# Turning an attention mask over in one transposing transfer instead of four, in a planned two-layer graph-attention kernel

## The chip, the cores and the metric

The kernel runs on one core of one Trainium2 chip. The metric is device time in microseconds (us) for one launch, the median of three timed runs. Five engines work side by side and are ordered only by semaphores: PE (TensorE, matrix products), DVE (VectorE), ACT (ScalarE), POOL (GpSimd) and SP (SyncE, which here only issues transfers). Matrix products read SBUF and write PSUM; DMA engines move data between HBM and SBUF, and within SBUF.

## The reference

There are 32 independent graphs of 512 nodes with 512 features, each with its own 512x512 adjacency matrix. Layer 0 is one head of graph attention, layer 1 holds two (four heads of 256 features, then one of 512); both have a layer norm and a relu in front and add to their input.

```python
h = relu(layernorm(x))                                  # layer 0
scores = leaky_relu(h@w_src [:,None] + h@w_dst [None,:] + b)
scores = where(adj + eye == 0, -inf, scores)
x = x + softmax(scores, -1) @ h

h = relu(layernorm(x))                                  # layer 1
def gat_layer(x, mask, W, a_src, a_dst, bias):
    xl = x @ W                                          # per head
    e = leaky_relu(asrc[:, None] + adst[None, :])       # [source, target]
    e = where(mask, e, -1e9)
    return softmax(e, axis=source).T @ xl + bias
h = elu(gat_layer(h, mask, W1, ...))                    # 4 heads x 256, side by side
x = x + gat_layer(h, mask, W2, ...)                     # 1 head x 512
```

Every softmax needs the mask twice: once with the node that is summed over along the free axis, to find each target's largest score, and once with it on the partitions, to mask the weights that the matrix product takes. So each graph's mask is used in both orientations, in both layers (layer 0 and layer 1 prepare masks of their own).

## The kernel before

A graph's nodes lie on the 128 partitions in `T` = 4 blocks; most tiles are 128 x 4 x 512. All 32 graphs go through the same steps, and a graph's layer 0 is worked on while the graph before it is in layer 1.

**The planner.** Nothing is issued directly. Each step is entered with `op(engines, cost, emit, reads, writes, ahead, lock)` (L60) in the order of the program text. `Plan.run` (L88) then makes schedules ("drafts") in Python before the kernel is built, and emits the instructions in the order of the best one. A draft (L132) is a list schedule: each engine takes, of the steps whose inputs are ready by the plan's own costs, the one of lowest rank. The rank of step i is at first `i - ahead` (L86): `AHEAD` = 400 pulls a step forward, `-LATER` = -300 puts it back. After a draft, `latest` (L112) works out how late each step could have been, and that is the rank for the next draft; up to `DRAFTS` = 6 are made in this chain, and the one with the earliest end by the plan's own costs is kept. `lock` marks steps on DVE and POOL that the plan does not overlap. Costs stand in `on_dve`, `on_pool`, `by_dma`, `by_turning` and so on (L234 to L264). On the chip each engine runs its instructions strictly in the planned order, and waits on semaphores.

**The masks.** `masks0` (L719) loads a graph's adjacency matrix with one POOL-issued transfer (`load_adj`, L706) that casts to bf16, turns it into 0 or a large negative number on DVE (L726, L729), and has it turned over by `transposed_mask` (L711): four transposing transfers issued from SP (L715), one for each block of 128 source nodes. `masks1` does the same for layer 1 (L741, L747). The buffers are `m0`, `m0T`, `m1`, `m1T` (128 x 4 x 512, bf16). In `edge_weights` (L625) DVE adds a mask row to the scores and takes the maximum (L634; with `m0` in layer 0, with `m1T` in layer 1), PE spreads that maximum over the partitions (L497), ACT makes the scores `E` (L655), DVE subtracts the maximum (L658), POOL adds the other mask (L660; `m0T` in layer 0, `m1` in layer 1) and ACT takes the exponential (L663). The products of `E` with the values are `aggregate` (L666, PE at L673).

**Rows by way of HBM.** A score vector is turned into a row on all partitions by a PE transpose (L596), a copy (L530), a transfer to HBM (`lines<-row`, L602) and a broadcasting transfer back (`row<-lines`, L612), both on SP's queue, then sometimes a copy to PSUM (L622).

**The projections** (`products`, L816, PE at L868) multiply in quarters by a seven-product scheme. Their weights are four quarters and four combinations T1, T2, T3, -T4 of them, made once in `sums` (L473, instructions at L480 and L481) after the weights have come in and after `scores_1` and `scores_2` (L439, L452, DVE dots at L383) have put two score columns beside each quarter. `weights_of` (L486) tells which pieces a product waits for.

**The beginning and the end.** The first lines of the plan (L1043 on) load graph 0's features, the constants, and go through layer 0 of graph 0. At the end, `EARLY` = T // 2 = 2 of the four output blocks of the last graph but one are entered ahead of the last graph's heads (L1060), the other two behind its last projection (L1076), and then the last graph's own output.

## Time and profile before

| | |
|---|---|
| median of 3 timed runs | 3653.59 us (3653.02 to 3653.67) |
| the profiled execution | 3651.96 us, of which 3650.2 us lie between its first and last instruction (the span) |
| mean granted TensorE clock | 0.993 |
| PE busy | 3534.9 us, 97% of the span |
| DVE busy | 2870.0 us, 79% |
| ACT busy | 2253.6 us, 62% |
| POOL busy | 1494.5 us, 41% |
| transposing transfers of masks | 256, four for each of 64 masks, 131 KB each |
| transposing transfers of head outputs (`turned`, L556) | 192, 262 KB each |

Times in the profile are counted from the first instruction. A group line names the source line, the engine, the operation, what it writes and reads, its shape and how often it ran, then its busy time in us and the mean ns of one, then how long the engine stood idle just before such instructions and what ended that. PE is the engine that is busy nearly all of the time.

### The profile page before, as it was taken

The numbers are of one execution on the slowest core, as the hardware profiler recorded it, in microseconds if no ns is written. First come the engines' busy times: TensorE is split into PE (matmuls) and PEld (weight loads), VectorE is DVE, ScalarE is ACT, GpSimd is POOL, SyncE is SP. The second block draws the span as 40 slices with busy tenths as digits, with TensorE's granted clock in tenths as the row PEclk, the third lists the DMA queues.
The fourth block names the chain that finished last, engine by engine and source line by source line (L and its number), as shares of the span: only waits on it lengthen the run. The fifth ranks groups of instructions, "written<-read, shape, count | busy, mean of one in ns | idle before, by whom it ended". The sixth has DMA issues, their size and how long they took to land.

```text
span 3650.2 us, 50711 instructions
## 1 busy us (share of the span) xinstructions
PE 3534.9 (97%) x16852; PEld 3039.1 (83%) x16852; DVE 2870.0 (79%) x7341; ACT 2253.6 (62%) x3929; POOL 1494.5 (41%) x1297
## 2 busy tenths in 40 slices
PE   4899999999999999999999999999999999999998
PEld 3688888888888888888888888888888888888877
DVE  7978778878778887778787788777787877887855
ACT  2666566665666665666656566656666656666554
POOL 4534334434334443344343344343343433443422
PEclk9999999999999999999999999999999999999999
DMA  6244333444333443434443344443344433334321
GB/s 165 72 116 116 99 100 103 94 128 113 95 94 105 104 122 105 96 96 105 116 115 100 93 104 99 124 111 92 98 110 105 118 99 101 101 99 122 102 76 40
DMA packets 516519, 378.85 MB, mean 104 GB/s; under 512 B 354488, under 2 KB 393120, under 8 KB 516256
## 3 DMA queue, kind: packets, MB, share of 16 engines
q1 hardware_dynamic: 482464, 342.06, 33.2%
q0 software_dynamic: 33792, 33.56, 6.5%
q8 instruction: 132, 2.16, 0.2%
q14 instruction: 131, 1.07, 0.1%
HBM read 257.16 MB, written 68.01 MB: 89 GB/s over the span
## 4 chain that ended last, share of the span: by engine, by line
PE 75%; DVE 12%; POOL 4%; ACT 2%; issue 2%; DMA 1%; SPq 1%; DVEq 0%; POOLq 0%; ACTq 0%
PE acc L673 42%; PE acc L868 28%; DVE junk L383 4%; PE acc L497 4%; POOL E_one L660 4%; DVE junk L634 2%; DVE E L849 1%; ACT acc L622 1%; DVE E_one L658 1%; DVE hT L536 1%; DMA row<-lines 1%; DVE col L512 1%; ACT h L520 1%; PE acc L596 1%; SPq L715 1%
## 5 line engine op out<-in xcount | busy, mean ns | idle before, releaser
L673 PE MATMUL acc<-pair,E 128*128 128x257 f32 x4096 | 915.9, 379 | 2.8 <-ACT E L663 2.8
L673 PEld LDWEIGHTS acc<-pair,E 128*128 128x128 f32 x4096 | 771.2, 189 | 115.7 <-ACT E L663 3.2
L660 POOL TENSOR_TENSOR E<-E,m 128x512 f32<-128x512 f32 x512 | 619.7, 1239 | 461.7 <-DVE E L658 451.4
L868 PE MATMUL acc<-w_T,E 128*128 128x257 f32 (+1 forms) x2048 | 526.3, 381 | 5.3 <-POOL w_T L481 5.3
L673 PE MATMUL acc<-h,E_one 128*128 128x256 f32 (+1 forms) x2048 | 485.8, 381 | 9.1 <-ACT E_one L663 6.5
L634 DVE CUSTOM_DVE_ANT_0 junk<-m1T,acc 128x512 bf16<-128x512 bf16 x640 | 435.7, 681 | 30.3 <-ACT acc L622 14.9
L673 PE MATMUL acc<-xl,E_one 128*128 128x257 f32 x1984 | 447.8, 380 | 3.9 <-ACT E_one L663 3.3
L868 PEld LDWEIGHTS acc<-w_T,E 128*128 128x128 f32 x2048 | 384.5, 190 | 63.8 <-POOL w_T L481 5.7
L673 PEld LDWEIGHTS acc<-h,E_one 128*128 128x128 f32 x2048 | 379.6, 190 | 64.2 <-ACT E_one L663 8.5
L881 DVE TENSOR_TENSOR pair<-acc,pair 128x258 f32<-128x258 f32 (+1 forms) x390 | 165.8, 426 | 330.8 <-PE acc L868 285.7
L673 PEld LDWEIGHTS acc<-xl,E_one 128*128 128x128 f32 x1984 | 370.1, 190 | 58.8 <-ACT E_one L663 8.6
L663 ACT ACTIVATE E<-E 128x512 f32<-128x512 f32 x512 | 314.8, 621 | 123.2 <-POOL E L660 123.1
L530 ACT COPY pair<-acc 128x258 f32<-128x258 f32 (+1 forms) x456 | 168.9, 371 | 314.1 <-PE acc L868 308.8
L655 ACT ACTIVATE E<-row,ac 128x512 f32<-128x512 f32 x512 | 340.4, 709 | 32.9 <-DMA row<-lines 32.3
L658 DVE TENSOR_TENSOR E<-E,acc 128x512 f32<-128x512 f32 x512 | 327.5, 676 | 13.1 <-PE acc L497 12.7
L530 ACT COPY xl<-acc 128x257 f32<-128x257 f32 x220 | 81.3, 370 | 388.5 <-PE acc L868 388.5
L660 POOL TENSOR_TENSOR E_one<-E_one,m0T 128x512 f32<-128x512 f32 x128 | 144.7, 1154 | 339.6 <-DVE E_one L658 339.6
L709 POOL DMA_DIRECT2D m<-in_adj_dram x64 | 51.5, 804 | 540.5 <-DVE col L634 493.7
L868 PE MATMUL acc<-w,hT 128*128 128x258 f32 x1024 | 267.7, 382 | 0.0
L868 PE MATMUL acc<-w,E 128*128 128x257 f32 (+1 forms) x1024 | 258.0, 380 | 0.0
L941 DVE SCALAR_TENSOR_TENSOR v<-acc,r,b_r 128x256 f32<-128x256 f32 x512 | 241.8, 478 | 9.0
L868 PE MATMUL acc<-w,pair 128*128 128x257 f32 x1024 | 248.3, 379 | 0.0
(114 smaller groups left out, 6167.2 us busy)
## 6 DMA issues: line engine op xcount, KB each, us to landing
row<-lines SPq DMA_DIRECT2D x442, 256.0 KB
m<-in_adj_dram POOLq DMA_DIRECT2D x64, 512.0 KB, 5.8
x<-in_x_dram SPq DMA_DIRECT2D x32, 1024.0 KB
spill<-x SPq DMA_DIRECT2D x32, 1024.0 KB
x<-spill SPq DMA_DIRECT2D x32, 1024.0 KB
out_dram<-x SPq DMA_DIRECT2D x30, 1024.0 KB
v<-row SPq DMA_TRANSPOSE x192
m0T<-m SPq DMA_TRANSPOSE x128
```

Source lines behind the costliest of these rows:

```text
L383: nc.vector.scalar_tensor_tensor(junk[:, : vector.shape[1]], values, 1.0, vector, op0=ALU.mult, op1=ALU.mult, accum_out=out)
L497: op("PE", on_pe(P, transpose=True), lambda: nc.tensor.transpose(dst_of(), src_of(), identity), src, dst(part), ahead)
L530: nc.scalar.copy(dst_of(), src_of())
L634: lambda t=t: nc.vector.tensor_tensor_reduce(junk, mask_max.at[:, t, :], a_row.at, 1.0, LOWEST, ALU.add, ALU.max, accum_out=amax.at[:, t : ...
L655: lambda t=t: nc.scalar.activation(E.at[:, t, :], c_row.at, AF.Prelu, bias=a_of(t), scale=1.0, alpha=SLOPE),
L658: op("DVE", on_dve(N), lambda t=t: nc.vector.tensor_sub(E.at[:, t, :], E.at[:, t, :], m_row.at), m_row(*ROW) + E(t), E(t))
L660: "POOL", on_pool(N, True), lambda t=t: nc.gpsimd.tensor_add(E.at[:, t, :], E.at[:, t, :], mask.at[:, t, :]),
L663: op("ACT", on_act(N), lambda t=t: nc.scalar.activation(E.at[:, t, :], E.at[:, t, :], AF.Exp), E(t), E(t))
L673: lambda s=s: nc.tensor.matmul(acc.at[:, :n], E.at[:, s, node_block(t)], of(s), start=(s == 0), stop=(s == T - 1)),
L868: lambda k=k: nc.tensor.matmul(acc.at[:, :width], at[a]()[:, k, node_block(r)], weight_of(w, k, c), start=(first and k == 0), stop=(k == n ...
L881: op("DVE", on_dve(width), lambda: nc.vector.tensor_add(place(), acc.at[:, :width], place()), acc(0) + token, token)
L941: lambda i=i, v=v, acc=acc, r=r: nc.vector.scalar_tensor_tensor(v.at[:, i, :], acc.at[:, :F], r.at, b1_r[:, h * F : (h + 1) * F], op0=ALU. ...
```

## The change

It has six parts.

1. `transposed_mask` turns the whole 128 x 2048 mask with one transfer (both callers pass `True`). The result then lies in another order: of each 128-column block of the turned mask, the four source blocks are no longer side by side. `mask_row` picks the row out as four pieces of 128, and the two users (L634, L660) get their operands as 128 x 4 x 128 by `by_blocks`.
2. `load_adj` keeps every later adjacency load waiting for the first one to have landed (`START`), and its planned costs differ for the first three.
3. `load_x(0)` gets a higher rank, ahead of the constants.
4. `sums` is made in two pieces: the weight values as soon as the weights are in, and the two score columns (8 elements a partition for W1) when the dots are done. That is eight instructions for each of the two weight matrices instead of four.
5. `EARLY` is 1: one block of the last graph but one is entered ahead of the last graph's heads, three behind its projection.
6. The planner keeps `ahead` apart from `i` and tries six multiples of it (0.25 to 1.5), and makes two drafts of each (one by the rank, one by `latest`) in place of a chain of up to six.

```diff
-    DRAFTS = 6
+    AHEAD, DRAFTS = (0.25, 0.5, 0.75, 1.0, 1.25, 1.5), 1
...
-        self.ops.append((engines, cost, emit, after, bufs, i - ahead, lock))
+        self.ops.append((engines, cost, emit, after, bufs, (i, ahead), lock))
...
-        rank, best = [o[5] for o in self.ops], None
-        for _ in range(self.DRAFTS):
-            draft = self.draft(rank)
-            if draft is None:
-                break
-            if best is None or draft.end < best.end:
-                best = draft
-            rank = self.latest(draft)
+        best = None
+        for part in self.AHEAD:
+            draft = self.draft([i - part * ahead for i, ahead in (o[5] for o in self.ops)])
+            for _ in range(self.DRAFTS):
+                if draft is not None and (best is None or draft.end < best.end):
+                    best = draft
+                draft = draft and self.draft(self.latest(draft))
...
-    def sums(w, name, kinds, n, later):
+    def sums(w, name, nk, kinds, n, later):
-        for dst, a, b_ in (("T3", "22", "T1"), ("T1", "T1", "11"), ("T2", "22", "T1"), ("-T4", "21", "T2")):
-            token = {q: W[name](*((q, *kind) for kind in kinds)) + W[name]((q, "done")) for q in FACTORS}
...
+        for part, cols in (("values", slice(2, None)), ("columns", slice(0, 2))):
+            token = {
+                q: W[name]((q, part), *((q, k) for k in range(nk)), *((q, *kind) for kind in kinds if part == "columns"))
+                for q in FACTORS
+            }
+            for dst, a, b_ in (("T3", "22", "T1"), ("T1", "T1", "11"), ("T2", "22", "T1"), ("-T4", "21", "T2")):
+                width = n if part == "values" else 16
...
     def weights_of(name, kinds):
-        return lambda q: W[name](*((q, *kind) for kind in kinds)) + W[name]((q, "done"))
+        return lambda q: W[name](*((q, *kind) for kind in kinds), (q, "values"), (q, "columns"))
...
-                    junk, mask_max.at[:, t, :], a_row.at, 1.0, LOWEST, ALU.add, ALU.max, accum_out=amax.at[:, t : t + 1]
+                    by_blocks(junk), mask_row(mask_max, t), by_blocks(a_row.at), 1.0, LOWEST, ALU.add, ALU.max,
+                    accum_out=amax.at[:, t : t + 1],
...
-                "POOL", on_pool(N, True), lambda t=t: nc.gpsimd.tensor_add(E.at[:, t, :], E.at[:, t, :], mask.at[:, t, :]),
+                lambda t=t: nc.gpsimd.tensor_add(by_blocks(E.at[:, t, :]), by_blocks(E.at[:, t, :]), mask_row(mask, t)),
...
+    START, adj_loads = Buffer(None), []
...
-            (), xb(*((t, half) for t in range(T) for half in range(2))),
+            (), xb(*((t, half) for t in range(T) for half in range(2))), 0 if b else 2 * AHEAD,
...
-        op("POOL", (2200.0, 8000.0), lambda: nc.gpsimd.dma_start(m.at, node_tiles(adj, b)), (), m(*ROW))
-    def transposed_mask(m, mT):
-        for t in range(T):
+        first, early = not START.wrote, len(adj_loads) < 3
+        adj_loads.append(b)
+        op(
+            "POOL", (1100.0, 5500.0) if first else (2200.0, 16000.0 if early else 8000.0), lambda: nc.gpsimd.dma_start(m.at, node_tiles(adj, b)),
+            () if first else START(0), m(*ROW) + (START(0) if first else []),
+        )
+    def transposed_mask(m, mT, whole=False):
+        for t in (None,) if whole else ROW:
             op(
-                "SP", by_turning(2 * P * N),
-                lambda t=t: nc.sync.dma_start(mT.at[:, :, node_block(t)], m.at[:, t, :], transpose=True),
-                m(t), mT(t),
+                "SP", by_turning(2 * P * N * (T if whole else 1)),
+                lambda t=t: nc.sync.dma_start(
+                    mT.at.rearrange("p a (b n) -> p (a b) n", n=P) if whole else mT.at[:, :, node_block(t)],
+                    m.at.rearrange("p t n -> p (t n)") if whole else m.at[:, t, :], transpose=True,
+                ),
+                m(*ROW) if whole else m(t), mT(*ROW) if whole else mT(t),
             )
+    def by_blocks(row):
+        return row.rearrange("p (b n) -> p b n", n=P)
+    def mask_row(mask, t):
+        if mask.kind in ("m0T", "m1T"):
+            return mask.at.rearrange("p a (b n) -> p a b n", n=P)[:, :, t, :]
+        return by_blocks(mask.at[:, t, :])
...
-    EARLY = T // 2
+    EARLY = 1
```

## The prediction

> **What bounds the kernel now.** I read the busy shares first, then busy time by stretch, then PE's waits, then the timeline of the beginning, one graph in the middle and the end.
>
> ```profile
> PE 3534.9 (97%) x16852; PEld 3039.1 (83%) x16852; DVE 2870.0 (79%) x7341; ACT 2253.6 (62%) x3929; POOL 1494.5 (41%) x1297
> ...
> 0.00:60.00 60.00, 20.35 (x76) 15.90 (x76) 43.38 (x143) 9.15 (x13) 14.10 (x22) 1.00 0.90 208
> 60.00:120.00 60.00, 39.67 (x151) 31.59 (x152) 54.33 (x140) 24.75 (x51) 34.12 (x20) 0.74 0.32 91
> 120.00:200.00 80.00, 77.49 (x373) 66.89 (x372) 67.97 (x174) 51.93 (x86) 37.24 (x31) 1.00 0.26 73
> ...
> 1000.00:1500.00 500.00, 494.89 (x2374) 427.24 (x2373) 401.37 (x1025) 320.62 (x550) 209.31 (x182) 1.00 0.40 104
> ...
> 3600.00:3650.20 50.20, 39.31 (x171) 32.61 (x169) 14.39 (x34) 7.48 (x16) 6.63 (x6) 0.90 0.06 21
> ```
>
> In the stretches the columns are length, busy PE, weight loads, DVE, ACT, POOL, then granted clock, DMA share, GB/s. The number of matrix products is not changed, so time can only come from PE's idle time, 3650.2 - 3534.9 = 115 us, and from stretches at a low clock. Of the 115, 39.6 + 20.3 = 60 us lie in the first 120 us, 2.5 us up to 200 us, about 34 us in the 3200 us up to 3400, and 19 us behind that. So the beginning is the largest pool, the middle is a small loss per graph times some 29 graphs, and the end is third.
>
> PE's waits say what ends last in each. First the beginning (up to 120 us), then the middle (120 to 3400):
>
> ```profile
> PE acc L497 <- DVE junk L383: 24.9, 4, 21.7
> PE acc L497 <- DVE col L641: 8.4, 2, 4.3
> PE acc L868 <- POOL w_T L481: 5.3, 1, 5.3
> PE acc L868 <- DVE pair L881: 5.0, 1, 5.0
> ...
> PE acc L497 <- ACT acc L622: 26.0, 26, 1.2
> PE acc L596 <- DVE ac L766: 4.2, 22, 0.5
> ```
>
> Columns: total us, times, longest. In the beginning PE waits for DVE, which is 90 to 100% busy in each 10 us slice from 20 to 80 us; DVE itself can't start before the features are there. In the middle there is one recurring gap of about 1 us a graph. None of PE's long waits in the middle names a mask's landing; in all waits together DVE's L634 waits 1.5 us, in 2 instances, for L715. The four-transfer turning is already hidden there, so part 1 can pay only through what it takes from SP's queue and by letting the plan be laid out differently.
>
> **Part 1, one transfer for four.** The two transposing rows have different sizes, 131 KB and 262 KB:
>
> ```profile
> L715 SPq DMA_TRANSPOSE m0T<-m x128: 1192/1259/2693, 24.5 to 3325.6; - x128
> L715 SPq DMA_TRANSPOSE m1T<-m x128: 1188/1194/3186, 35.8 to 3538.6; - x128
> ...
> L556 SPq DMA_TRANSPOSE v<-row x192: 1231/1232/2468, 134.2 to 3589.9; - x192
> ```
>
> These are min/median/max ns that SP spends on one. Twice the bytes cost 40 ns more, so four times cost some 120 ns: 1.3 us (estimate from these rows). SP spends 4 x 1.25 = 5.0 us on a mask now and 1.3 us after, 2 x 3.7 = 7.4 us less a graph. The data: the quiet 262 KB transfer issued at 262.45 us moves nothing up to 263.60 and has the DMA engines full (228 GB/s) from 263.60 to 264.75; a quiet 131 KB one keeps them at 0.81 for 0.70 us (187 GB/s). So 0.6 us and 1.1 us, hence about 2.0 us for the whole mask, and landing 1.2 + 2.0 = 3.2 us after issue, where the fourth of four lands 3 x 1.26 + 1.2 + 0.6 = 5.6 us after the first issue. Gain 2.4 us in the mask's own latency, hidden in the middle. The row transfers behind it on SP's queue (L612, which release ACT's L622 and L655) can go out up to 3.7 us sooner, but stand behind 2.0 us of data and not 0.6.
>
> The strided operands: L634 takes 681 to 685 ns (768 of them), L660 with m0T 1154 ns (128 of them). No row shows the same instruction with four pieces of 128. The nearest are DVE's and POOL's sums at L849 and L850, whose operands are two pieces of 256: on hT DVE takes 676 ns, the same as the unbroken L658 (676), and POOL's 1306 to 1487 stands beside 1288 for the unbroken L796. So I take 0 on both, with bounds of 0 and 0.2 us on each of 128 POOL instructions (POOL is 41% busy, so it costs only where a chain waits), and 0 to 30 ns on DVE: 768 x 0.03 = 23 us on an engine with 780 us free.
>
> In the middle, the recurring gap is at L497 (the spread of the maximum), for example 1.09 us before 553.43. There L641 took 0.80 us instead of 0.15 and L639 1.01, while POOL's four L660 ran from 548.75 to 553.25; ahead of that DVE's first L634 with m1T started at 545.92, released by L622 (0.60 us idle), whose row left SP at 542.56 behind the four m1T transfers of 535.78 to 542.45. With one transfer that row can leave about 3 us sooner, and the maximum can be done before POOL's block begins. If so 26 x 1.0 = 26 us go; if the new order puts DVE's instructions as they are now, nothing; if it makes another such gap, 26 to 30 us come. Between ends of -28 and +28 I take -8, about a third of the gain, because the gap depends on DVE's order, which follows the plan and not the transfer.
>
> **Parts 2 and 3, the beginning.** DVE idles until x lands:
>
> ```profile
> DVE st L503 <- DMA x<-in_x_dram: 12.4, 1, 12.4
> ...
> 0.00:5.00 5.00, 0.00 (x0) 0.00 (x0) 0.25 (x4) 0.00 (x0) 3.31 (x13) 1.00 0.57 87
> 5.00:10.00 5.00, 0.00 (x0) 0.00 (x0) 0.00 (x0) 0.00 (x0) 0.00 (x0) 1.00 1.09 242
> 10.00:14.00 4.00, 0.00 (x0) 0.00 (x0) 0.02 (x1) 0.00 (x0) 0.00 (x0) 1.00 1.13 314
> ```
>
> By 14 us the queues had moved 5 x 87 + 5 x 242 + 4 x 314 KB = 2.9 MB, of which x is 1.05 MB. Beside it ran three adjacency loads (0.52 MB each as written) and two constant rows (0.26 MB each). With x first (0.75 instead of 2.14 us) and one adjacency load beside it, 1.57 MB are to be moved. The same curve reaches that at 9.7 us, 1.4 us of which go with the earlier issue: x lands at about 8.3, 5.7 us sooner than the 13.98 at which DVE starts now. DVE is full from 20 us on, so its whole sequence moves up if its other inputs are in time. I take -5 us, bounds 0 (another load is late instead: w1 and the attention vectors, whose dots fill DVE from 35 to 62 us) and -7. The later adjacency loads wait on POOL's queue until the first has landed; behind them there stand only L904 and, at 17.28 us, L507. DVE takes the layer-1 mask at 18.94 us now, but its first reader (L634) comes at 107.31, and the second layer-0 mask at 55.26.
>
> **Part 4, the sums.** Now L481 runs on POOL at 70.27, 76.39 and 80.82 (2.8 us each) and PE stands 5.34 us until 79.25 for it; the eight products that follow took 3.81 us and not 1.74, in a slice with clock 0.77. Made from the values alone, the sums can run before DVE's dots end at 65.3. PE saves 5.3 + 2.1 us there, unless DVE is then late with what comes next: it is 96% busy in that slice. The four column pieces add four instructions of about 0.1 us each, per matrix. DVE's dots beside POOL took 1.6 to 2.7 us instead of 0.69 from 67 to 84 us, and one beside the first L481 took 2.46 at 43.77; that blocking is moved into the dots, not removed. I take -4, bounds -8 and +3.
>
> The Trainium skill, "SBUF — State Buffer", says in its part on the port that DVE and GpSimd share that a vector instruction with two SBUF inputs and a GpSimd instruction that reads SBUF exclude each other for their whole length; that agrees with the 2.46 us above and speaks against part 4: by it the sums only exchange places with dots, DVE gains nothing, and the part would be worth 0 instead of -4, the time 3639.
>
> **Part 5, the end.** PE is idle 10.9 us in the last 50, mostly 3.0 us before 3626.08 and 2.7 us before 3629.94, while the last maximum is taken. One block is 16 products of 0.22 us, 3.5 us of filler. But filler runs wherever PE would wait, and DVE is 88 to 98% busy from 3550 to 3580, so some goes there. I take -2, bounds -3.5 and +1.
>
> **Part 6, the drafts.** It costs nothing itself. It decides the order, and so is in the bounds of the middle.
>
> Sum: -8 - 5 - 4 - 2 = -19 us on the profiled 3651.96: 3633. The median of the timed runs stands 1.6 us above the profiled execution: 3634.6, so 3635.
>
> **The rivals.** *The middle's gap goes whole*: L497's 26 us vanish, -26 - 11 = -37: 3617. For it: the gap is one and the same in 26 graphs, so one change of order removes all. Against: two releasers stand within 0.1 us of each other before 553.43 (L641 and L622), and both must move. *The beginning is hidden*: DVE is full anyway and its dots, blocked by POOL, end when they did; the middle stays: -2 to -3, 3651. For it: DVE's load in the first 120 us is 98 us. Against: 12.4 us of its idle time are the wait for x. *Slower, the new draft leaves a second gap*: only one refinement follows each start now, where six were chained. A second stall like L497's, 1.09 us in each of 28 graphs, is +30.5, less 11 from beginning and end: +19.5, 3673. It decides from 11 / 28 = 0.4 us a graph, and is slower by over 0.2% from 0.65. For it: middle gaps come from order alone, and the plan's costs don't hold such blocking of small DVE steps. Against: twelve drafts are compared, the first two of the old chain among them.
>
> **How the numbers follow.** Chances: forecast 0.49 (own range 3622 to 3646), the gap gone 0.17, hidden 0.16, slower 0.18. 0.2% is 7.3 us, about what a measurement of this kernel can tell from no change. Faster 0.49 + 0.17 = 0.66, same 0.16, slower 0.18. The range reaches from 3606 (gap gone and the better bounds of beginning and end) to 3664 (a second gap of some 0.75 us a graph); most of the slower rival is left out.
>
> **What would show it.** Right: BN_STATS starts near 8.3 us; the wait of L868 for L481 is gone; 64 transfers at L715 of about 1.3 us; L634 stays near 683 ns; L622 releases PE less. Wrong: L634 over 720 ns, PE idle over 1.6 us a graph in the middle, or the first L673 product later than 35 us (38.80 now).

## The result

| | before | after |
|---|---|---|
| median of 12 timed runs, side by side | 3652.94 us (3652.00 to 3654.26) | 3648.74 us (3645.19 to 3651.69) |
| span of the profiled execution | 3650.2 us | 3646.7 us |
| SP's time on the mask's transfers, each (median) | 4 x 1.19 to 1.26 us | 1.62 us (`m0T`), 3.03 us (`m1T`) |

The ratio is 0.9989, interval 0.9981 to 0.9996: 4.2 us or 0.11% faster. The interval lies just below 1, but one short measurement could not tell this from no change, and it is 14 us behind the forecast of 3635. The runs of the changed kernel lie 6.5 us apart, those of the kernel before 2.3.

The busy shares, and busy time by stretch (length, PE, weight loads, DVE, ACT, POOL, granted clock, DMA share, GB/s), of the changed kernel:

```profile
PE 3542.6 (97%) x16852; PEld 3036.1 (83%) x16852; DVE 2851.2 (78%) x7367; ACT 2264.6 (62%) x3929; POOL 1424.6 (39%) x1279
```

```profile
0.00:60.00 60.00, 24.18 (x94) 19.43 (x95) 41.88 (x125) 13.49 (x20) 27.44 (x29) 0.95 0.80 203
60.00:120.00 60.00, 44.44 (x179) 35.23 (x178) 55.30 (x172) 23.33 (x49) 28.16 (x25) 0.85 0.34 100
120.00:200.00 80.00, 72.85 (x339) 60.39 (x338) 66.53 (x167) 50.13 (x82) 34.19 (x29) 0.98 0.25 71
1000.00:1500.00 500.00, 495.13 (x2372) 425.74 (x2372) 401.31 (x1032) 325.42 (x554) 195.56 (x177) 1.00 0.38 103
```

PE is busier in the first 120 us (24.18 + 44.44 = 68.6 us, 60.0 before) and less busy from 120 to 200 (72.85, 77.49 before). In the middle nothing moves (495.13, 494.89 before).

For a sharper count I use PE's **lost time**. Consecutive products of 256 columns or more start 0.2175 us apart when nothing is in the way, those of 128 columns half of that, 0.1088 us; the 16852 products make 3503.1 us in every kernel here, and what a span has above that is lost, to waits, to a low clock or to the last output. It is put down to the stretch in which it falls. Each row is one profiled execution; the ratio is that of the timed runs to those of the kernel before on the same chip.

| kernel | lost, 0 to 200 us | 200 to 3400 | from 3400 | span | ratio (95%) |
|---|---|---|---|---|---|
| before | 78.1 | 43.5 | 25.5 | 3650.2 | |
| after | 76.0 | 43.1 | 24.5 | 3646.7 | 0.9989 (0.9981 to 0.9996) |
| e1: part 1 alone | 82.9 | 44.3 | 23.0 | 3653.2 | 0.9995 (0.9986 to 1.0003) |
| e2: parts 2 and 3 alone | 76.9 | 45.8 | 26.9 | 3652.7 | 0.9993 (0.9984 to 1.0002) |
| e3: part 4 alone | 79.6 | 45.1 | 26.6 | 3654.4 | 1.0002 (0.9993 to 1.0011) |
| e4: part 6 alone | 77.7 | 49.8 | 26.3 | 3657.0 | 0.9995 (0.9986 to 1.0004) |
| e5: first landing planned at 13000 | 75.1 | 38.5 | 23.7 | 3640.5 | 0.9959 (0.9947 to 0.9972) |
| e6: a real wait for the first landing | 77.9 | 42.2 | 22.5 | 3645.8 | one run |
| e7: two blocks held back | 77.6 | 43.3 | 22.0 | 3646.0 | 0.9975 (0.9965 to 0.9985) |
| e8: dots planned longer | 71.6 | 75.0 | 24.6 | 3674.4 | 1.0034 (1.0021 to 1.0046) |
| e9: short dots | 65.5 | 41.9 | 21.7 | 3632.2 | 0.9949 (0.9934 to 0.9964) |
| e10: e5 and e7 | 75.3 | 38.9 | 21.0 | 3638.4 | 0.9946 (0.9933 to 0.9958) |
| e11: part 1 undone, drawn anew | 77.8 | 45.4 | 26.1 | 3652.4 | 0.9993 (0.9984 to 1.0002) |
| e12: first landing planned at 9000 | 74.6 | 30.7 | 22.9 | 3631.3 | 0.9936 (0.9920 to 0.9953) |
| e13: e12's order, four transfers | 75.5 | 79.0 | 26.2 | 3683.9 | 1.0055 (1.0043 to 1.0068) |
| e14: e12 and e7 | 73.3 | 31.0 | 20.8 | 3628.2 | 0.9923 (0.9911 to 0.9936) |
| e15: after's order, four transfers | 77.6 | 56.1 | 25.6 | 3662.4 | 1.0018 (1.0010 to 1.0027) |

So the 3.5 us between the two profiled spans are 2.1 from the beginning, 0.4 from the middle and 1.0 from the end. Some profiled executions lie off their kernel's median: e13's 8.6 us above it, e8's 11.4, e4's 4.4, e5's, e7's and e10's 3, and e9's 3.8 below. So a stretch is read for where the time lies, and what a kernel gains by the ratio.

What ends PE's waits after the change, in the beginning (up to 120 us) and in the middle (120 to 3400); line numbers have moved (L497 is now L506, L596 L605, L622 L631, L673 L684, L868 L900, L481 L488):

```profile
PE acc L506 <- DVE junk L384: 21.9, 4, 18.8
PE acc L605 <- DVE ac L798: 9.3, 1, 9.3
PE acc L684 <- ACT E_one L674: 7.5, 2, 4.1
...
PE acc L900 <- POOL w_T L488: 0.8, 1, 0.8
```

```profile
PE acc L506 <- DVE col L651: 16.3, 28, 0.7
PE acc L506 <- DVE v L1013: 8.7, 29, 1.9
PE acc L684 <- ACT row L987: 2.4, 1, 2.4
```

Both waits that the prediction named are gone as such: the 5.3 us for the sums are 0.8, and no wait at L506 for ACT's L631 is left of the 26.0 us. In their places stand one of 9.3 us for a score step of the next graph (L798), and 16.3 + 8.7 us at the same L506 for two of DVE's steps.

### The profile page after: what moved, and what is told of

It reads as the page before. It is cut to its first block, busy times and chain, and to the rows that moved or that the text cites. A ratio compares the mean times of both kernels' runs of the same rounds, so it can differ in the third digit from the quotient of the medians.

```text
span 3646.7 us, 50543 instructions
## 1 busy us (share of the span) xinstructions
PE 3542.6 (97%) x16852; PEld 3036.1 (83%) x16852; DVE 2851.2 (78%) x7367; ACT 2264.6 (62%) x3929; POOL 1424.6 (39%) x1279
## 4 chain that ended last, share of the span: by engine, by line
PE 80%; DVE 14%; ACT 2%; issue 1%; DMA 1%; POOL 0%; DVEq 0%; ACTq 0%; SPq 0%
PE acc L684 45%; PE acc L900 32%; DVE junk L384 5%; PE acc L506 3%; DVE v L1013 1%; DVE hT L881 1%; DVE hT L545 1%; DVE col L521 1%; DVE col L649 1%; ACT h L529 1%; DVE v L973 1%; PE acc L605 1%; DVE junk L643 1%; DVE E L881 1%; DVE xl L913 1%
## 5 line engine op out<-in xcount | busy, mean ns | idle before, releaser
L684 PE MATMUL acc<-pair,E 128*128 128x257 f32 x4096 | 920.4, 379 | 2.4 <-ACT row L987 2.4
L684 PEld LDWEIGHTS acc<-pair,E 128*128 128x128 f32 x4096 | 771.7, 189 | 115.5 <-ACT row L987 2.8
L671 POOL TENSOR_TENSOR E<-E,m 128x512 f32<-128x512 f32 x512 | 605.1, 1211 | 455.3 <-DVE E L668 396.7
L900 PE MATMUL acc<-w_T,E 128*128 128x257 f32 (+1 forms) x2048 | 517.9, 380 | 0.8 <-POOL w_T L488 0.8
L684 PE MATMUL acc<-h,E_one 128*128 128x256 f32 (+1 forms) x2048 | 491.2, 381 | 8.6 <-ACT E_one L674 7.5
L684 PE MATMUL acc<-xl,E_one 128*128 128x257 f32 x1984 | 447.9, 381 | 2.7 <-ACT E_one L674 2.7
L643 DVE CUSTOM_DVE_ANT_0 junk<-m1T,acc 128x512 bf16<-128x512 bf16 x640 | 436.6, 682 | 11.4 <-PE acc L506 3.4
L900 PEld LDWEIGHTS acc<-w_T,E 128*128 128x128 f32 x2048 | 385.4, 189 | 61.0 <-POOL w_T L488 1.5
L684 PEld LDWEIGHTS acc<-h,E_one 128*128 128x128 f32 x2048 | 380.8, 191 | 63.6 <-ACT E_one L674 8.3
L684 PEld LDWEIGHTS acc<-xl,E_one 128*128 128x128 f32 x1984 | 371.8, 190 | 54.7 <-ACT E_one L674 3.1
L674 ACT ACTIVATE E<-E 128x512 f32<-128x512 f32 x512 | 315.6, 623 | 161.7 <-POOL E L671 161.4
L665 ACT ACTIVATE E<-row,ac 128x512 f32<-128x512 f32 x512 | 341.1, 707 | 2.4 <-DMA row<-lines 2.4
L671 POOL TENSOR_TENSOR E_one<-E_one,m0T 128x512 f32<-128x512 f32 x128 | 144.4, 1152 | 355.6 <-DVE E_one L668 355.6
L900 PE MATMUL acc<-w,hT 128*128 128x258 f32 x1024 | 265.5, 384 | 0.6 <-issue 0.5
L900 PE MATMUL acc<-w,E 128*128 128x257 f32 (+1 forms) x1024 | 264.2, 380 | 0.0
L702 DVE SCALAR_TENSOR_TENSOR x<-acc,r,x 128x256 f32<-128x256 f32 x512 | 239.7, 479 | 30.9 <-PE acc L684 22.8
L529 ACT ACTIVATE h<-x,col,col 128x512 f32<-128x512 f32 x256 | 187.6, 804 | 109.0 <-DVE col L521 109.0
L539 ACT COPY xl<-acc 128x257 f32<-128x257 f32 x218 | 77.6, 369 | 284.9 <-PE acc L900 284.8
```

The lines of the kernel that those rows point to most:

```text
L529: lambda: nc.scalar.activation(h.at[:, t, :D], X.at[:, t, :], AF.Relu, bias=nmr.at[:, t : t + 1], scale=rstd.at[:, t : t + 1]),
L539: nc.scalar.copy(dst_of(), src_of())
L643: lambda t=t: nc.vector.tensor_tensor_reduce(by_blocks(junk), mask_row(mask_max, t), by_blocks(a_row.at), 1.0, LOWEST, ALU.add, ALU.max, a ...
L665: lambda t=t: nc.scalar.activation(E.at[:, t, :], c_row.at, AF.Prelu, bias=a_of(t), scale=1.0, alpha=SLOPE),
L671: lambda t=t: nc.gpsimd.tensor_add(by_blocks(E.at[:, t, :]), by_blocks(E.at[:, t, :]), mask_row(mask, t)),
L674: op("ACT", on_act(N), lambda t=t: nc.scalar.activation(E.at[:, t, :], E.at[:, t, :], AF.Exp), E(t), E(t))
```

## The experiments

**e1 to e4: the parts one by one**, each put into the kernel before. One line stands here for each of the four edits, in the order e1 to e4; the rest of each is the same part of the change's diff.

```diff
-        transposed_mask(m0, m0T)
+        transposed_mask(m0, m0T, True)
...
+    START, adj_loads = Buffer(None), []
...
+        for part, cols in (("values", slice(2, None)), ("columns", slice(0, 2))):
...
-    DRAFTS = 6
+    AHEAD, DRAFTS = (0.25, 0.5, 0.75, 1.0, 1.25, 1.5), 1
```

> Part 1 alone (one transposing transfer a mask, strided operands; beginning, sums, end and drafts as before). PE's lost time is the span less 0.2175 us for each product of 256 columns or more and 0.109 us for each smaller one: 78.0 us up to 200 us, 43.5 us from 200 to 3400 and 25.5 us behind that in the kernel before, 147.0 in all; 76.0, 43.1 and 24.5, 143.6 in all, in the changed one. Theory (the turning is hidden, and the middle's loss per graph only moves from one wait to another when the order changes): median within 4 us of before, 3649 to 3657; lost from 200 to 3400 us 38 to 50; L634 stays at 680 to 686 ns. Rival A (SP's freed queue time is worth something in the middle): 3645 or less, with the middle's loss under 36. Rival B (the strided operands or the larger transfer cost): 3658 or more, with L634 over 700 ns or waits of DVE or POOL on the mask transfer.

> Parts 2 and 3 alone (first features ahead of the constants, planned costs and planned order of the adjacency loads), all else as before. Theory (the features come 8 us earlier, but the plan takes the first adjacency load to land 5.5 us after its issue where the chip needs 12.7, and DVE's order puts the mask's additions in front of the last statistics): statistics start near 6 us, DVE then stands 4 to 6 us for the adjacency landing, first aggregation product at 32 to 35 us (38.80 before), and PE's loss up to 200 us falls by 1 to 4 us from 78; median 3648 to 3654. Rival A (the features were hidden by DVE's load anyway): first product at 37 us or later, loss unchanged. Rival B (features pay in full): first product at 31 us or earlier and loss up to 200 us of 72 or less, median 3647 or less.

> Part 4 alone (sums in two pieces), all else as before. Theory (the value sums leave the path, but the score columns still wait for the last of DVE's 32 dots, and the POOL sums only exchange places with dots that they block): the wait of PE for POOL's sums of 5.3 us falls under 1.5 us, and PE's loss up to 200 us stays within 3 us of 78; median 3650 to 3656. Rival (the sums were on the path): loss up to 200 us 74 or less, median 3649 or less.

> Part 6 alone (six multiples of ahead, two drafts of each, in place of a chain of six), all else as before. Theory (drafts only lay the order out differently, and one order loses about as much per graph as another): loss from 200 to 3400 us 35 to 55 (43.5 before), loss up to 200 us 73 to 83; median 3646 to 3660. Rival A (the old chain's later drafts were the better ones, a second gap per graph appears): middle's loss over 60, median over 3665. Rival B (the new drafts take the middle's recurring wait away): middle's loss under 25, median under 3640.

None of the four can be told from no change (ratios 0.9993 to 1.0002); part 5 was not run alone. Part 1 alone swaps the middle's wait as the whole change does (L497 for `col` L642 14.4 us and for `v` L996 7.8 us, none for L622), at no gain. Parts 2 and 3 alone bring the first aggregation product from 38.80 to 32.58 us, and the start loses 76.9 us instead of 78.1. Part 4 alone has no wait for the sums left among PE's longest, but 11.8 us at L505 for an ACT step and 7.6 us at L604 for DVE (L505 and L604 are L497 and L596 there). e2, e3 and e4 all keep the middle's gap behind the row's copy: 28.4, 24.1 and 26.8 us.

**e5, e6: the start's loads.** In the changed kernel the features land early, but DVE's next step is late. DVE's waits up to 120 us, and its timeline (start, duration, idle before and its releaser in brackets):

```profile
DVE m L758 <- DMA m<-in_adj_dram: 5.5, 1, 5.5
DVE st L512 <- DMA x<-in_x_dram: 4.4, 1, 4.4
```

```profile
5.99 1.29 DVE L512 BATCH_NORM_STATS2 st<-x 128x6 f32<-128x512 f32 x2 [4.39 <-DMA x<-in_x_dram]
...
8.51 0.17 DVE L513 BATCH_NORM_AGGREGATE mv<-st 128x2 f32<-128x6 f32 x1
14.18 0.29 DVE L758 TENSOR_TENSOR m<-m,ident 128x128 bf16<-128x128 bf16 x1 [5.51 <-DMA m<-in_adj_dram]
14.39 0.17 DVE L513 BATCH_NORM_AGGREGATE mv<-st 128x2 f32<-128x6 f32 x1
```

The features are there at 5.99 us (13.98 before). But the plan takes the first adjacency load for 5.5 us long and has put a mask step ahead of the layer norm's last one; issued at 1.51 us, the load released DVE at 14.18, after 12.7 us. e5 plans 13000 ns; e6 makes the later loads wait on POOL for the first one to land, which the change does only in its plan (below). The first pair of lines is e5's edit, the rest e6's.

```diff
-            "POOL", (1100.0, 5500.0) if first else (2200.0, 16000.0 if early else 8000.0), lambda: nc.gpsimd.dma_start(m.at, node_tiles(adj, b)),
+            "POOL", (1100.0, 13000.0) if first else (2200.0, 16000.0 if early else 8000.0), lambda: nc.gpsimd.dma_start(m.at, node_tiles(adj, b)),
...
+        held = early and not first and m.kind == "m1"
+
+        def load():
+            if held:
+                nc.gpsimd.tensor_copy(m.at[:, 0, :2], adj_loads[0].at[:, 0, :2])
+            nc.gpsimd.dma_start(m.at, node_tiles(adj, b))
```

> The changed kernel with one number of the plan altered: the first adjacency load is taken to land 13.0 us after its issue instead of 5.5. DVE's order then has all of the layer norm and the eight score dots of graph 0 ahead of the mask's additions. Theory (the earlier features were eaten by DVE standing 5.5 us for the mask in the middle of the statistics): DVE's wait for the adjacency load falls under 1 us, the first aggregation product comes at 27 to 30 us (33.59 in the changed kernel, 38.80 before) and PE's loss up to 200 us falls from 76.0 to 69 to 74; median 3 to 6 us below the changed kernel, 0.15 to 0.3% below before. Rival (what comes behind is set by the 32 weight dots and their loads, not by the first chain): first product earlier all the same, but the first projection product no earlier than 58 us (59.2 in the changed kernel) and loss 75 or more.

> The changed kernel with the order of the adjacency loads made a real wait: each of the two layer-1 masks that are loaded early is first touched on POOL by a copy of two elements from the first mask, so their loads are issued only when the first has landed. The order of all instructions is the same otherwise. Theory (the three loads go one after the other in their queue anyway, and the first shares the engines with SP's constants): the first mask's landing stays within 1.5 us of 14.18, the first aggregation product within 1.5 us of 33.59. Rival (the two others take the first one's share): landing at 10 us or earlier, first product at 30 us or earlier.

e5: ratio 0.9959. But its gain isn't in the start: the first aggregation product comes 12 us later than in the changed kernel (45.70 against 33.59) and the start still loses only 0.9 us less; the middle loses 4.6 us less. DVE is even busier there (102.3 of the first 120 us, 97.2 in the changed kernel). So the first chain of steps does not set what the start loses. e6: DVE waits 5.3 us for the first mask as before, and the time is the changed kernel's (3647.57). By this one run the real wait is worth nothing: the three loads pass through the queue one after another without it too (packets of 6.31 to 13.13, 13.04 to 17.46 and 17.37 to 22.12 us in the changed kernel; 5.42 to 11.0, 10.9 to 17.2 and 17.1 to 22.8 before).

**e7: the kept-back blocks.** The last 46.7 us hold the two waits of before still, 3.0 us and 2.7 us, because the three blocks kept back are used up by 3591 us.

```diff
-    layer2_out(B - 2, ROW[EARLY:], False)
+    layer2_out(B - 2, ROW[EARLY:2], False)
+    layer2_out(B - 2, ROW[2:], False, HELD)
```

`HELD` is the last projection's scores: in the plan, the products of these two blocks now need them.

> The changed kernel with two of the three blocks that part 5 keeps back made to depend, in the plan, on the last projection's scores, so that they stand in PE's order in the two waits of the last softmax (3.0 and 2.7 us). Theory (kept-back blocks are used up in the stretch in which DVE is late with the last graph's heads; in the tail PE waits for 5.7 us whatever EARLY is): PE's loss behind 3400 us falls from 24.5 to 18 to 21, the waits of 3.0 and 2.7 us shrink to under 1 us each, median 3 to 6 us below the changed kernel. Rival (the heads' stretch loses what the tail gains): loss behind 3400 us within 1.5 us of 24.5.

PE's waits from 3400 us on, in the changed kernel and in e7:

```profile
PE acc L684 <- ACT E_one L674: 5.4, 2, 2.7
PE acc L506 <- DVE col L651: 3.0, 1, 3.0
PE acc L506 <- DVE v L1013: 1.2, 1, 1.2
```

```profile
PE acc L506 <- DVE v L1013: 3.4, 2, 2.1
PE acc L684 <- ACT E_one L674: 2.7, 1, 2.7
PE acc L506 <- DVE col L651: 1.5, 1, 1.5
```

The loss behind 3600 us falls from 14.9 to 5.7 us, but between 3550 and 3600, where the blocks had been used, it grows from 1.3 to 8.5. Filler taken from one hole opens another; 2.5 us of 9.2 stay.

**e8: the dots planned 130 ns longer**, as long as the chip takes for them.

```diff
+def on_dot(n):
+    one = n / 0.96 + 200.0
+    return one, one + 85.0
...
-                        "DVE", on_dve(F),
+                        "DVE", on_dot(F),
```

The same exchange stands at the three other kinds of dots.

> The changed kernel with DVE's dots planned 130 ns longer (0.47 us for 256 elements and 0.73 for 512; the trace has 0.47 and 0.77 from one to the next). Theory (PE stands 9.3 us at 73 us behind the transpose of graph 1's scores because the plan takes DVE to be done sooner than it is): that wait falls under 4 us and PE's loss from 60 to 80 us from 13.6 to under 10, the loss up to 200 us from 76.0 to 70 to 74. Rival (POOL's blocking of DVE, which the plan's lock does not get right, makes DVE late): a wait of PE of 6 us or more for DVE's dots remains between 55 and 85 us, loss up to 200 us 75 or more.

The start loses the least of all plans with whole dots (71.6), and the middle 75.0. PE's waits there (200 to 3400 us):

```profile
PE acc L689 <- ACT E_one L679: 45.6, 24, 2.2
```

L689 and L679 are L684 and L674 of the changed kernel. That is the second gap of the slower rival, some 2 us in 24 graphs, made by a number in the plan and by nothing else. By the ratios the kernel is 0.45% or 16 us slower than the changed one.

**e9: does DVE's work set the start?**

```diff
+    def short(values, vector, out):
+        dot(values[:, :8], vector[:, :8], out)
...
-                        lambda w=w1_s[q][:, kk, h // 2, :], i=i, h=h: dot(
+                        lambda w=w1_s[q][:, kk, h // 2, :], i=i, h=h: short(
```

`scores_2` uses it in the same way.

> The changed kernel with its plan and order untouched, but the 64 dots that make the score columns of both weight matrices read 8 features each instead of all (256, 380 or 132): the score columns are not the reference's. What is left out is DVE time at the start only, some 64 x 0.3 us = 19 us, more where POOL blocks a dot (some of them took 1.6 us and more). Theory 'DVE's total work sets the start': PE's lost time in the first 200 us falls from 76.0 to 64 or less, most of it from the wait of the matrix products on L384 (21.9 us) and the wait for L798 (9.3 us), and the time falls by 10 to 20 us, to 3629-3639. Rival 'the loads and the first graph's own chain of steps set the start, DVE's dots only fill the time': lost time 73 or more, time 3645-3650. The middle and the end stay (43 and 24 us) by both, as the order is the same.

A dot takes 168 ns in the median instead of 426, so 64 x 0.26 = 16.5 us of DVE's work are gone; the start loses 10.5 us less (65.5), and the time is 3637.81, ratio 0.9949. The named waits did not shrink (L384 21.4 us, L798 9.4 us), so the expectation had the right engine and the wrong place: of the 10.5 us, 5.4 are won from 120 to 140 us and 2.9 from 100 to 120, the rest is small and goes both ways. Not all of that is waiting: from 100 to 140 us the changed kernel has 20 products at about twice their usual distance, 4.3 us in all, under a granted clock of 0.83 and 0.91, and e9, where the clock is 1.00, has none. That the clock followed from the shorter waits was not tried. Still, less work on DVE shortens the start where an earlier first chain did not. The same can be read in the two kernels. DVE was busy 97.7 of the first 120 us before and 97.2 after: all that the early features bring to DVE is idle time in another place. But DVE's work is not all that counts: e8 differs from the changed kernel by its order alone, has DVE as busy in the first 200 us (163.3 and 163.7 us), and loses 4.4 us less there.

**e10: e5 and e7 together.**

> The two edits to the changed kernel's plan that gained most, together: the first adjacency load planned at 13000 ns instead of 5500 (e5_honest_landing, -9.6 us against the changed kernel) and two of the three kept-back blocks of the last graph but one held in the plan behind the last projection's scores (e7_held_blocks, -3.9 us). Theory 'gains of the plan's order do not add: each edit makes another plan, and the middle is drawn anew with it': the middle's lost time is anywhere from 38 to 50 us, and the time from 3634 to 3652. Rival 'they add': start 75, middle 38.5, end 21 to 22, time 3636 to 3638, and the tail behind 3600 us at some 6 us.

75.3, 38.9 and 21.0 us; ratio 0.9946. They add, as the rival said: holding the blocks leaves e5's order as it is up to the last part.

**e11: part 1 undone in the changed kernel**, the plan drawn for four transfers.

```diff
-        transposed_mask(m0, m0T, True)
+        transposed_mask(m0, m0T)
...
-        transposed_mask(m1, m1T, True)
+        transposed_mask(m1, m1T)
...
-        if mask.kind in ("m0T", "m1T"):
-            return mask.at.rearrange("p a (b n) -> p a b n", n=P)[:, :, t, :]
```

> The changed kernel with part 1 alone undone: four transposing transfers a mask again, all else as changed. Theory 'the single transfer matters only through the plan's order in the middle': SP has its queue busy 4 us more for each mask, but PE's gap stays between 1.2 and 1.7 us a graph; the gap at L506 is released by ACT's L631 again (as in the kernel before and with parts 2 and 3 or part 6 alone) and the middle loses 40 to 52 us; start 73-80, end 22-27; time 3643 to 3658. Rival 'the whole transfer's saving on SP's queue is worth what the forecast put on the middle, and another part gave it back': the middle loses 52 us or more, time 3658 or longer.

Ratio 0.9993, the middle at 45.4, and PE's first wait in the middle is the old one again (L506 for ACT's L631, 24.0 us, 24 times). A plan made for four transfers hides them as well as the changed kernel's plan hides one.

**e12: between 5500 and 13000.**

```diff
-            "POOL", (1100.0, 5500.0) if first else (2200.0, 16000.0 if early else 8000.0), lambda: nc.gpsimd.dma_start(m.at, node_tiles(adj, b)),
+            "POOL", (1100.0, 9000.0) if first else (2200.0, 16000.0 if early else 8000.0), lambda: nc.gpsimd.dma_start(m.at, node_tiles(adj, b)),
```

> The changed kernel with the first adjacency load planned at 9000 ns, between the 5500 as changed and the 13000 of e5_honest_landing; nothing else differs. Theory 'the number only draws another order, and the middle is better or worse by no rule': the middle's lost time lies outside of what runs between the two (38.5 and 43.1 us), so below 37 or above 45, and the time is below 3637 or above 3650. Rival 'the gain of e5 came from the number being nearer to the truth, and half the way brings some of it': start 74 to 77, middle 38 to 43, time 3639 to 3646, and PE's wait at L684 for ACT's L674 shows in some of the graphs.

3633.64 us, ratio 0.9936, the middle at 30.7, far outside of 38.5 to 43.1. Of the waits of PE that are long enough to be listed from 200 to 3400 us this line is all that is left; below it stands the wait that DVE has instead:

```profile
PE acc L684 <- ACT E_one L674: 4.7, 6, 1.3
```

```profile
DVE junk L643 <- ACT acc L631: 35.6, 28, 1.3
```

One planned time of one transfer at the very beginning takes the gap out of 28 graphs, because it draws another order from the first products on. The theory of a new drawing stands, and the rival, that a truer number brings the gain by degrees, falls: 5500, 9000 and 13000 give 43.1, 30.7 and 38.5. In the changed kernel DVE has the same wait for the copied row ahead of another step, `pair`:

```profile
DVE pair L913 <- ACT acc L631: 38.5, 29, 2.1
```

In before, after, e1 to e4, e11 and e15, which all have a gap at L497 or L506, DVE stands ahead of `pair` for 35 to 39 us; in e5 and e12, which have none, ahead of L643. That goes together; that it is the cause was not tried.

**e13, e15: one order, four transfers.** All runs without the single transfer so far had another order too. Here the planned step stays, and SP issues four in its place.

```diff
-                lambda t=t: nc.sync.dma_start(
-                    mT.at.rearrange("p a (b n) -> p (a b) n", n=P) if whole else mT.at[:, :, node_block(t)],
-                    m.at.rearrange("p t n -> p (t n)") if whole else m.at[:, t, :], transpose=True,
-                ),
+                lambda t=t: [
+                    nc.sync.dma_start(by_blocks(mT.at[:, s, :]), m.at[:, s, :], transpose=True) for s in ROW
+                ],
```

> The kernel of e12_landing_9000 with every engine's order kept, but in each place where SP issues one whole transposing transfer it issues four, of one source block each, one behind the other. SP is held 4 x 1.2 us instead of 1.6 to 3.0, and the rows behind it go out some 2 to 3 us later. Theory 'the order is all, the single transfer is hidden': the middle's lost time is 29 to 34 us (30.7 with one), the time within 4 us of e12, 3632 to 3638. Rival 'the order is gapless only because SP is free sooner': the gap comes back, 0.4 to 1.1 us in each of 28 graphs, the middle at 42 us or more, the time 3645 or more, and PE's waits in the middle name a row's copy (ACT's L630) or a mask row's step (DVE's L642).

> The changed kernel with its order kept, but four transposing transfers issued in each place of the one. Theory 'the order is all, the single transfer is hidden': start 75 to 79, middle 41 to 46, end 24 to 25, time within 4 us of the changed kernel's 3648.7. Rival 'the single transfer is worth the 3 us of SP's queue a graph that the forecast counted': the recurring gaps at L506 grow by 0.3 us or more a graph, the middle to 52 us or more, the time to 3657 or more.

My theory, that the order is all, fell in both. In e12's order the middle goes from 30.7 to 79.0 us and the time to 3677.12; in the changed kernel's from 43.1 to 56.1, and to 3664.33. In size that is what the rivals said, but not in place: PE's new waits are neither for the row's copy or the mask row's step (e13) nor longer gaps at L506 (e15), but at L684, behind ACT. By the ratios, which leave out that the kernels were timed on different chips, four transfers in place of one cost 43 us in the one order and 11 in the other. SP's timeline for one graph, of the changed kernel and of e15:

```profile
1088.92 0.32 SPq L621 DMA_DIRECT2D row<-lines  x1
1089.29 3.28 SPq L735 DMA_TRANSPOSE m1T<-m  x1
1092.62 0.91 SPq L611 DMA_DIRECT2D lines<-row  x2
...
1099.81 1.62 SPq L735 DMA_TRANSPOSE m0T<-m  x1
1101.53 0.52 SPq L621 DMA_DIRECT2D row<-lines  x1
```

```profile
1095.18 0.32 SPq L621 DMA_DIRECT2D row<-lines  x1
1095.55 5.15 SPq L736 DMA_TRANSPOSE m1T<-m  x4
1100.75 0.90 SPq L611 DMA_DIRECT2D lines<-row  x2
...
1105.75 5.12 SPq L736 DMA_TRANSPOSE m0T<-m  x4
1110.97 0.52 SPq L621 DMA_DIRECT2D row<-lines  x1
```

The row transfers behind a mask go out 1.9 and 3.5 us later. Those rows are what ACT waits for in e13 (200 to 3400 us), and PE waits behind ACT:

```profile
ACT acc L631 <- DMA row<-lines: 115.1, 101, 5.9
```

```profile
PE acc L684 <- ACT E_one L674: 34.5, 36, 3.5
```

e12 has 29.6 us in 46 such waits at L631. In e15 ACT waits 99.7 us for rows where the changed kernel has 14.8 (12.4 at L631, 2.4 at L665), while PE's gaps at L506 stay about as they were (21.2 us, 23.1 in the changed kernel) and none of them is for L631. First ACT, then PE in e15 (200 to 3400 us):

```profile
ACT acc L631 <- DMA row<-lines: 60.4, 54, 5.1
ACT E L665 <- DMA row<-lines: 39.3, 30, 3.2
```

```profile
PE acc L506 <- DVE col L651: 14.5, 22, 1.6
PE acc L506 <- DVE v L1012: 6.7, 28, 0.3
PE acc L684 <- ACT E_one L674: 6.4, 11, 1.5
```

So the single transfer matters where the order relies on it, and nearly not at all where the plan has laid the work out round four (e11).

**e14: e12 and e7 together**, the version to which the runs point.

> The kernel of e12_landing_9000 with two of the three kept-back blocks held in the plan behind the last projection's scores, as in e7_held_blocks. The order differs from e12's in the last 110 us alone. Theory 'a change that leaves the order before it alone adds its own gain': start 74.6 and middle 30.7 stay within 1.5 us, the end falls from 22.9 to 20-21, time 3630 to 3634. Rival 'the end is bounded by the last chain, and what is held is lost earlier': the end stays at 22 to 24, time 3633 to 3637.

3629.74 us (3628.95 to 3631.48), ratio 0.9923: 28 us faster than the kernel before, nearly seven times the gain of the change as made. By the profile the start loses 73.3, the middle 31.0 and the end 20.8 us.

## Why the prediction was wrong

**Bounds.** Where the time is (beginning, middle, end) and what PE waits for there was read rightly, and each stretch gave way to something: the beginning loses 65.5 us in e9 (78.1 before), the middle 30.7 in e12 (43.5), the end 20.8 in e14 (25.5). What failed is what the change would take of them: in the profiled executions 0.4 us came in the middle where 8 were forecast, 2.1 in the beginning where 9 were (parts 2, 3 and 4), 1.0 at the end where 2 were.

**Part 1, "-8, about a third of the gain": the first step that failed.** Half of its mechanism stands: rows behind a shorter transfer on SP go out sooner, and where the order is held, four transfers cost 11 us (e15) or 43 (e13). The other half does not: that L631 no longer releases PE is the new order's doing and not the earlier row's, for in e15, in the same order, four transfers do not bring that wait back. The change lets the plan be drawn anew, and the new drawing has other gaps of about the same size at the same place: 0.4 us came, not 8. What the single transfer would bring in the order of the kernel before was not run. The bounds of -28 and +28 were the truer statement. The reason given, "the gap depends on DVE's order, which follows the plan and not the transfer", spoke against any size between the bounds; a third of the gain had nothing behind it.

**SP's time, "1.3 us"**: too low. The two sizes that the profile before had (131 KB at 1.19 to 1.26, 262 KB at 1.23) showed hardly any growth, but 524 KB does:

```profile
L735 SPq DMA_TRANSPOSE m0T<-m x32: 1506/1618/7914, 17.4 to 3319.1; - x32
L735 SPq DMA_TRANSPOSE m1T<-m x32: 1564/3032/5042, 79.2 to 3528.7; - x32
```

The saving is 3.5 + 1.9 = 5.4 us a graph and not 7.4. The landing 3.2 us after the issue is right for `m0T` (median 3.2), not for `m1T` (4.6).

**Strided operands, 0**: right.

```profile
L643 DVE CUSTOM_DVE_ANT_0 junk<-m1T,acc x640: 665/686/691, 104.4 to 3621.1; 128x512 bf16<-128x512 bf16 x160
...
L671 POOL TENSOR_TENSOR E_one<-E_one,m0T x128: 1142/1148/1331, 31.7 to 3428.7; 128x512 f32<-128x512 f32 x128
```

In the average L643 takes 682 ns with `m1T` and 685 with `m`, where it took 681 and 685 before (as L634), and L671 1152 with `m0T`, where it took 1154 (as L660).

**Parts 2 and 3, -5, and part 4, -4: the second step that failed, "its whole sequence moves up".** The features were sized well enough (8.3 us expected, 5.99 measured), and the first aggregation product moved to 33.59 us, inside the 35 that were named as the test. The test was the wrong one: e5 has it at 45.70 and a better start. Up to 120 us PE's lost time fell by 10.0 us (75.1 to 65.1), a little more than the two terms; from 120 to 200 us it rose from 2.9 to 10.9, and 8.0 of the 10 were given back. There PE waits 7.1 us, 4.1 of them for steps of DVE and 3.0 for steps of ACT, and the granted clock is 0.91 from 120 to 140 us (1.00 before). The prediction wrote "DVE is full from 20 us on, so its whole sequence moves up if its other inputs are in time". They were not: 5.5 us of the gain became DVE's wait for the adjacency, and by 120 us DVE had been busy no longer than before. That is the rival "the beginning is hidden" (3651), which came closest; I gave it 0.16. Its reason, that DVE is full, is shown in part: e9 shows that DVE's work holds the start, e8 that the order alone moves it by 4.4 us. What holds the rest of it stays open.

A statement of fact in the change's description and in the prediction is wrong too: START keeps no load waiting on the chip. It writes no tile, so there is no semaphore behind it; POOL issues the next load at 2.54 us, right behind the first. It stands only in the plan, and in e6's one run a real wait does not help.

**Part 4 and the Trainium skill.** "SBUF — State Buffer", in its part on who interferes with whom, says that a vector instruction with two SBUF inputs contends with a GpSimd instruction that reads SBUF. The trace agrees, and shows what goes beside it. POOL makes four value sums from 42.33 to 51.93 us without a pause; in that time one of DVE's mask steps with two SBUF inputs lasted 2.10 us, to 52.07, where the two of its kind behind the sums took 0.27 and 0.26; the additions out of PSUM (L702) beside it took 0.47 or 0.48 each and the layer norm's statistics 0.66 to 0.68. By that page part 4 was to be worth 0; alone it gave +1.5 us in the start (e3), nearer to 0 than to my -4.

**Part 5, -2**: -1.0 in the end, within its bounds. But e1, without part 5, loses 2.5 us less there than the kernel before, so the 1.0 us can't be put down to this part. The doubt about it ("filler runs wherever PE would wait") is what e7 shows.

**Part 6, nothing by itself, in the middle's bounds**: right; alone 0.9995.

**The slower rival** did not come in the change, but e8 shows its mechanism. **The gap gone whole** came in e12, with 12.8 us off the middle instead of 26: PE's lost time without any long wait is still 31 us there, so half of the 26 us of waits at L497 came back in gaps too short to be listed. The range (3606 to 3664) held the time.

## What to carry to other kernels

Where a planner lays out the order, a change has two effects: what it costs or saves at one and the same order, and what the new drawing does. The second was larger here than any part (planned costs alone took the ratio from 0.9936 in e12 to 1.0034 in e8), so hold the order to price the first, and try a few drawings on the chip before a version is kept. And where one engine is nearly full in a stretch, an earlier start of its first chain can just move its idle time, as here: try first what the stretch gains when work is taken away from that engine, as e9 did.

## What the runs showed of the hardware

- A transposing transfer holds SP longer with its size, but not in proportion: 1.19 to 1.26 us for 131 KB, 1.23 for 262 KB, 1.62 for 524 KB, and 3.0 where, as with `m1T` above, it follows a row transfer on the queue within 0.1 us. It is the distance and not the tile: the two transfers of `m1T` that were issued 3.2 and 10 us behind one (at 79.2 and 3528.7 us) held SP 1.56 and 1.64 us. The data of `m0T` moved in 2.0 us, as estimated.
- The first adjacency load, 0.52 MB as written, took 12.7 us from issue to use beside the other loads of the beginning; three such loads issued back to back were moved one after another.
- DVE's dot over 8 features took 168 ns and over 256 features 426: by these two lengths more than a third of the longer dot's time does not depend on its length.
